# A four-layer convolution net on one core: the first image's reduce product, the bias tables and the loads at the first layer's two ends rearranged

## The chip, the cores and the metric

The kernel runs on one core of one Trainium2 chip. The metric is device time in microseconds of one execution. The engines are PE (matrix products, with PEld for its weight loads), DVE (vector), ACT (scalar), POOL (GpSimd) and SP (which here only issues DMAs). ACT and POOL issue DMAs too.

## The reference

The input is 4 images of 256 channels and 56 x 56 positions, float32. Four layers follow, each of the form x + layer(groupnorm(x)) with groups of 8 channels:

```
# layer 0 (involution): every position makes its own 7x7 kernel for each of 16 channel groups
h    = einsum('bchw,oc->bohw', xn, reduce_w) + reduce_b      # 256 -> 64 channels
kern = einsum('bchw,oc->bohw', h, span_w) + span_b           # 64 -> 49*16
out  = (kern * patches7x7(xn)).sum(axis=taps)                # 16 channels share a kernel

# layer 1: conv3x3, batch norm, relu, conv3x3, batch norm, + xn, relu
# layer 2: involution as in layer 0, with batch norm and relu after the reduce and after the sum
# layer 3: x * sigmoid(W @ first element) + x * spatial factor (both from FFTs' real parts)
```

## The kernel before

**Stages.** `involution_layer(0, ...)` does layer 0, `conv_layer` layer 1, and `involution_layer(2, ...)` layers 2 and 3. Between stages the images lie in DRAM (`stage`). Channels lie on the 128 partitions, so an image is two channel blocks `cb` of 128 x 3136 numbers, each in one of three rotating blocks of the tile named `xs` (`new_block`, L101). `new_h` (L104) gives the tile `hp`, which holds the 64 reduced channels twice, on partitions 0 to 63 and 64 to 127.

**Layer 0's units.** A unit is (image b, channel block cb), so there are eight, in order. Each has a tap phase and an output phase.

- The tap phase (`tap_matrices`, L460) runs 32 steps. A step has 6 matmuls on PE (L471) out of `z_sb` (the span weights spread over a window) and `hp`, then one eviction into `kt` that adds the bias table `zb_sb`: on DVE (L489, one instruction) or in every fourth step on ACT (L482, six instructions). `hooks` hold work to be emitted after a given step.
- The output phase (`apply`, L501) runs seven columns of 8 positions. A column has 56 matmuls (L513), evictions on ACT (L526) and DVE (L533), and an addition on POOL (L538). After each column `next_windows` (L371) transposes the strip for the third column ahead on PE (L381), ACT copies it to `xw` (L382), and three DMAs on SP and one on POOL shift it (L388, L390). `next_strip` (L345) makes the normalized strip on POOL (L364). `column_sums` (L925) takes statistics on DVE. `early` and `late` hold work placed before and after a column.

**Before the first unit.** SP loads the two blocks of image 0 in parts (`load_block`, L236). DVE takes statistics of seven chunks of each block (`sums`, L328-333). `norm_steps` (L190-213) turns them into a scale and a shift: an aggregate on DVE, two one-column matmuls with `gavg_sb` (L197, L208), small DVE steps, and `rsqrt_eps` (L137), which uses DVE and POOL. `bottleneck(0)` (L395) scales the reduce weights to `redn` (L404), makes the bias `hb` (L411-420), and multiplies (L433): for each chunk of 9 rows a half-wide matmul, two chunks side by side on the two halves, accumulated over the two channel blocks. ACT evicts a bank into one half of `hp` (L450), and DVE copies it to the other half (L441). `make_tables` (L277) loads the span and bias weights, spreads them with DVE copies (L300, L308), and makes `zb_sb` with 24 matmuls (L315) and one copy (L322). `batch_norms` (L159) folds the batch norm parameters with small DVE operations and powers on POOL.

Layer 2's tables are made in unit (0,0): `make_tables(..., nc.sync)` runs at hooks 3, 14 and 21, and `save` at 22 writes both to DRAM (L824, L825). Image 1's first block is loaded at hook 23.

**From layer 0 to layer 1.** After column 0 of the last unit `begin_conv` (L985) loads on SP the rows of image 0 for the first convolution chunk (`load_rows`, L976) and both blocks of the raw weights of the first convolution (L991). When the unit ends, the norm of its block is computed. `conv_layer` then zeroes the edges of `ph1` and `ph2` on POOL (L1079-1086), issues on ACT the loads of weight positions 0 and 5 (`row_weights`, L1046-1047), combines the raw weights on DVE (L1058-1065), normalizes the rows into four phases (`phases`, L1114, channel block 0 on ACT and 1 on DVE), transforms them on DVE (`transform`, L1136), and starts `conv1` (L1254).

**What sets the order.** The start is ordered by the framework's scheduler, which places an instruction by its dependencies and priority. From `since = mark()` on, `in_order(since)` binds each engine to the order of emission: the hooks and the lists decide. Each engine's queue is strictly in that order.

Of the kernel before, what the change touches and what calls it, by code (L numbers as in the profile page):

```python
# [16 lines left out]
P = 128  # L17
# [54 lines left out]
def net_kernel(  # L72
# [68 lines left out]
    def bn_fold(name, par, gamma, beta, mean, var, n):  # L141

        s = const.tile([P, n], F32, name=f"{name}_s")
        t = const.tile([P, n], F32, name=f"{name}_t")
        rsqrt_eps(s, par(var), BN_EPS)
        nc.vector.tensor_mul(s, s, par(gamma))
        nc.vector.tensor_mul(t, par(mean), s)
        nc.vector.tensor_sub(t, par(beta), t)
        return s, t

# [8 lines left out]
    def batch_norms():  # L159

        par_of = {}
# [8 lines left out]
        s1, t1 = bn_fold("bn1", by_channel, L1_G1, L1_B1, L1_M1, L1_V1, NB)  # L170
        s2, t2 = bn_fold("bn2", by_channel, L1_G2, L1_B2, L1_M2, L1_V2, NB)
        s4, t4 = bn_fold("bn4", by_channel, L2_G, L2_B, L2_M, L2_V, NB)
        s3, t3 = bn_fold("bn3", by_row, L2_G1, L2_B1, L2_M1, L2_V1, 1)

        s4_of = {}
        for n in (2, 4):
            s4_of[n] = const.tile([P, n, NB], F32, name=f"s4_{n}")
            for i in range(n):
                nc.vector.tensor_scalar_mul(s4_of[n][:, i, :], s4, par_of[n][:, i : i + 1])
        bn.update(par=par_of, s1=s1, t1=t1, s2=s2, t2=t2, s3=s3, t3=t3, s4=s4_of, t4=t4)  # L180
# [49 lines left out]


# [4 lines left out]
    def load_block(dst, block, parts=1):  # L236
        n = NCHUNK // parts
        for j in range(0, NCHUNK, n):
            at = slice(j * CR * W, min(j + n, NCHUNK) * CR * W)
            nc.sync.dma_start(dst[:, at], block[:, at])  # L240

    def involution_layer(layer, xin, xout, red, span, sb, xs_of, ahead=None, pending=None):

        with ExitStack() as es:
# [12 lines left out]
            def warm(n):  # L257

                ps = one_bank()
                for _ in range(n):  # L260
                    nc.tensor.matmul(ps[:, :P], ident_sb, ident_sb, start=True, stop=True)

            def load(b, cb, parts=1):
                xs_of[b, cb] = new_block()
                load_block(xs_of[b, cb], xin[b][cb], parts)

            for cb in range(NB):
                if (0, cb) not in xs_of:
                    load(0, cb, 3)

            red_sb = wpool.tile([P, NB, 2, R], F32, name="red_sb")
            for i in range(2):
                nc.scalar.dma_start(red_sb[:, :, i], red.rearrange("(cb p) r -> p cb r", p=P))
# [1288 lines left out]
```

## Time and profile before

| | |
|---|---|
| median of 3 runs | 1864.59 us (1862.81 to 1867.78) |
| profiled execution | 1861.41 us |
| its span in the trace | 1859.5 us, 55572 instructions |
| busy in the span | PE 1705.2 us (92%), DVE 1430.2 (77%), ACT 751.4 (40%), POOL 432.0 (23%) |
| moved by DMA | 215.67 MB, mean 116 GB/s |
| mean granted PE clock | 0.967 |

Layer 0 runs from the start to about 530 us; layer 1 follows, then layers 2 and 3. The page cuts the span into 40 slices of 46.5 us. In its rows a digit is the busy share in tenths, and PEclk is the clock granted to PE in tenths of full speed. In a timeline a line has start, duration, engine, source line, operation, output and input, how many instructions are merged (x), and in brackets the idle time of that engine before it and what ended it. A float32 matmul shows as two records.

### The profile page before, as it was taken

What the parts mean: (1) busy time and instruction counts of PE and PEld (TensorE: products, weight loads), DVE (VectorE), ACT (ScalarE), POOL (GpSimd) and SP (SyncE); (2) the same over time, 40 slices, a digit from 0 to 9 for tenths busy, and PEclk for the clock granted to TensorE, in tenths of its full rate; (3) what the DMA queues carried; (4) which work ended last, traced back from release to release, by engine and by line L of the source; (5) the groups of instructions that cost most, each with busy time, mean ns of one, the idle gap of its engine ahead of it and who ended that gap; (6) DMA issues with size and microseconds to landing.
All of it is one profiled execution on the core that took longest, in us unless ns stands there. A gap on an engine that the chain in (4) does not pass through costs nothing.

```text
span 1859.5 us, 55572 instructions
## 1 busy us (share of the span) xinstructions
PE 1705.2 (92%) x24028; PEld 1501.5 (81%) x24028; DVE 1430.2 (77%) x2824; ACT 751.4 (40%) x1662; POOL 432.0 (23%) x615
## 2 busy tenths in 40 slices
PE   5999999999859999999999999997989899898886
PEld 3888888888748988898899889985877887877874
DVE  5687778776668988998889888874777778778764
ACT  2445445454413222231232312113656556565543
POOL 2323433244210000000000000000000663672683
PEclk9999999999969999999999999998999999999985
DMA  3445544453543111120121111132433765763652
GB/s 100 150 147 178 154 121 138 156 154 106 159 129 101 41 62 61 61 68 25 61 71 58 51 48 33 54 122 63 154 129 127 207 209 174 201 213 118 196 164 75
DMA packets 65504, 215.67 MB, mean 116 GB/s; under 512 B 13487, under 2 KB 20444, under 8 KB 61420
## 3 DMA queue, kind: packets, MB, share of 16 engines
q1 hardware_dynamic: 44364, 141.60, 24.6%
q0 software_dynamic: 14848, 65.85, 10.9%
q10 hardware_dynamic: 6048, 4.68, 0.8%
q8 instruction: 189, 3.10, 0.7%
q14 instruction: 55, 0.45, 0.1%
HBM read 76.23 MB, written 49.15 MB: 67 GB/s over the span
## 4 chain that ended last, share of the span: by engine, by line
PE 67%; DVE 20%; DMA 4%; issue 3%; POOL 3%; ACT 2%; SPq 0%; DVEq 0%; POOLq 0%; ACTq 0%
PE mm L1336 20%; PE ps L513 15%; DVE kt L489 11%; PE mm L1254 10%; PE ps L471 8%; PE mm L1225 6%; PE ps L381 4%; DMA xw<-xw 2%; PE ps L433 2%; DVE un L533 2%; ACT hp L452 1%; DMA gx<-x 1%; PE ps L783 1%; DVE st L925 1%; DMA xs<-in_x_dram 1%
## 5 line engine op out<-in xcount | busy, mean ns | idle before, releaser
L513 PE MATMUL ps<-kt,xw 126*32 126x48 f32 (+1 forms) x12544 | 385.2, 236 | 57.0 <-DMA xw<-xw 19.2
L513 PEld LDWEIGHTS ps<-kt,xw 126*32 126x32 f32 (+1 forms) x12544 | 345.9, 122 | 102.6 <-issue 47.8
L471 PE MATMUL ps<-hp,z_sb 64*126 64x133 f32 x6144 | 387.2, 281 | 15.6 <-DVE kt L489 5.3
L471 PEld LDWEIGHTS ps<-hp,z_sb 64*126 64x126 f32 x6144 | 369.1, 188 | 30.4 <-DVE kt L489 6.6
L489 DVE TENSOR_TENSOR kt<-ps,zb_sb 126x798 f32<-126x798 f32 x384 | 357.8, 978 | 42.9 <-PE ps L471 42.4
L1336 PE MATMUL mm<-v,u_sb 128*128 128x280 f32 (+1 forms) x1728 | 383.2, 383 | 3.3 <-DVE v L1161 3.3
L1336 PEld LDWEIGHTS mm<-v,u_sb 128*128 128x128 f32 x1728 | 326.2, 189 | 57.4 <-DVE v L1161 3.6
L482 ACT ACTIVATE kt<-ps,zb_sb 126x133 f32<-126x133 f32 x768 | 224.0, 441 | 173.8 <-PE ps L471 173.8
L1254 PE MATMUL mm<-v,u_sb 128*128 128x252 f32 (+1 forms) x936 | 211.9, 387 | 12.6 <-DVE v L1145 12.6
L1254 PEld LDWEIGHTS mm<-v,u_sb 128*128 128x128 f32 x936 | 177.7, 191 | 43.1 <-issue 12.6
L533 DVE SCALAR_TENSOR_TENSOR un<-ps,par_sb,un 128x240 f32<-128x240 f32 x224 | 98.2, 456 | 101.9 <-ACT un L526 97.8
L533 DVE SCALAR_TENSOR_TENSOR un<-ps,s,un 128x240 f32<-128x240 f32 x224 | 102.4, 457 | 91.0 <-ACT un L528 86.7
L1373 POOL DMA_DIRECT2D x<-xs x24 | 13.1, 546 | 683.9 <-DVE xs L1372 538.6
L1321 ACT ACTIVATE res<-xs,shift,norm_sb 128x1120 f32<-128x1120 f32 (+1 forms) x24 | 30.2, 1259 | 234.8 <-DVE xs L1372 107.3
L538 POOL TENSOR_TENSOR xs<-un,xs 128x240 f32<-128x240 f32 x112 | 72.3, 665 | 223.0 <-DVE un L533 223.0
L382 ACT COPY xw<-ps 126x896 f32<-126x896 f32 x112 | 101.6, 907 | 50.1 <-PE ps L381 43.3
L381 PE MATMUL ps<-ident_sb,strip_sb 128*126 128x128 f32 x784 | 112.3, 284 | 1.4 <-DVE kt L489 0.8
L526 ACT ACTIVATE un<-ps,par_sb 128x240 f32<-128x240 f32 x112 | 50.1, 448 | 137.5 <-PE ps L513 134.9
L528 ACT ACTIVATE un<-ps,bn_t,s 128x240 f32<-128x240 f32 x112 | 60.1, 538 | 100.8 <-PE ps L513 94.6
L139 POOL TENSOR_TENSOR norm_sb<-norm_sb,mhalf 128x1 f32<-128x1 f32 x32 | 19.2, 602 | 351.0 <-DVE norm_sb L138 350.9
L1225 PE MATMUL mm<-xs,u_sb 128*128 128x126 f32 (+1 forms) x792 | 98.3, 277 | 1.3 <-DVE xs L1188 1.0
L1225 PEld LDWEIGHTS mm<-xs,u_sb 128*128 128x128 f32 x792 | 94.3, 191 | 2.7 <-issue 1.4
(224 smaller groups left out, 1962.3 us busy)
## 6 DMA issues: line engine op xcount, KB each, us to landing
xw<-xw SPq DMA_DIRECT2D x168, 252.0 KB
xw<-xw SPq DMA_DIRECT2D x224, 126.0 KB
xw<-xw POOLq DMA_DIRECT2D x56, 252.0 KB, 4.5
xs<-x SPq DMA_DIRECT2D x24, 560.0 KB
x<-xs POOLq DMA_DIRECT2D x8, 1568.0 KB, 8.1
xs<-x SPq DMA_DIRECT2D x8, 1568.0 KB
xs<-in_x_dram SPq DMA_DIRECT2D x6, 1568.0 KB
x<-xs SPq DMA_DIRECT2D x6, 1568.0 KB
```

The source lines that it names most:

```text
L381: nc.tensor.transpose(ps[:Q, k * P : (k + 1) * P], flat[:, k * Q : (k + 1) * Q], ident_sb)
L382: nc.scalar.copy(xw[:, :NSB, :], ps[:Q, : NSB * P].rearrange("q (n c) -> q n c", n=NSB))
L471: nc.tensor.matmul(ps[:Q, i, k * NT : (k + 1) * NT], z_sb[i * R : (i + 1) * R, cb * GB // 2 + gp, z0 : z0 + Q], hp[i * R : (i + 1) * R, py ...
L482: nc.scalar.activation(kt[:, g0 + i, pb, :, k], ps[:Q, i, k * NT : (k + 1) * NT], AF.Identity, bias=zb_sb[:, cb * GB + g0 + i, p0 + k : p0 ...
L489: nc.vector.tensor_tensor(kt[:, g0 : g0 + 2, pb], ps[:Q, :, : PB * NT].rearrange("q i (k t) -> q i t k", k=PB), zb_sb[:, cb * GB + g0 : cb ...
L513: nc.tensor.matmul(v[m * j : m * j + m, i, :, k * TP : (k + 1) * TP], xw[:, window(ty), m * j : m * j + m], kt[:, ng * j : ng * j + ng, :, ...
L528: nc.scalar.activation(part, o[0], AF.Identity, bias=bn["t4"][:, cb : cb + 1], scale=bn["s4"][ng][:, 0, cb : cb + 1])
L533: nc.vector.scalar_tensor_tensor(part, o[e], s, part, ALU.mult, ALU.add)
L538: nc.gpsimd.tensor_tensor(dst, u, dst, ALU.add)
L1225: nc.tensor.matmul(ps[:, co * m : (co + 1) * m], u[ci][:, co * P : (co + 1) * P], v2[:, e, : n // 2, ci * WT : (ci + 1) * WT], start=(ci = ...
L1254: nc.tensor.matmul(ps, u1_sb[:, ci, dy, k, co * P : (co + 1) * P], v[:, k, dy * NB + ci : (dy + n - 1) * NB + ci + 1 : NB, :], start=(j == 0),
L1336: nc.tensor.matmul(ps, u2_sb[:, ci, dy, k, co * P : (co + 1) * P], v[:, k, dy * NB + ci : (dy + n - 1) * NB + ci + 1 : NB, :], start=(j == 0),
```

## The change

- **Start.** A new generator, `begin`, runs in place of the two norms, `bottleneck(0)` and `make_tables`, now in a fixed order. The first tables come from POOL's DMA queue, with ACT making the copies and the 24 bias matmuls first on PE. Four and eight warm-up matmuls stand between the norm's matmuls. The 64-channel product is made 128 wide, by channel block: all seven chunks of block 0 into seven banks, then block 1 into the same banks. ACT evicts both halves at once, and no copies to the other half follow. The load of the image is in parts of 2, 2, 2 and 1 chunks for both blocks. The reduce weights are loaded on POOL's queue.
- **Parameters.** `batch_norms` is a generator. Two of its steps run in the start, and the rest at hooks 1, 2, 4, 6 and 7 of unit (0,0).
- **Layer 2's tables.** The span table is loaded at hook 16 of unit (3,0) and made by POOL, three copies after each of its columns 0 to 5. The bias table's matmuls run between the layers (`window_biases` in `conv_layer`).
- **Loads.** Image 1's first block is loaded at hook 16. The rows and the raw weights of channel block 1 are loaded on SP at hook 16 of unit (3,1), those of block 0 in three parts on ACT after its columns 0, 1 and 2. The loads of weight positions 0 and 5 move from ACT to SP.
- **Border.** The last block's norm moves into the first convolution stages (`slow`). All eight phases of the first chunk are made on ACT.

```diff
+    def bias_table(bias, sb, load, copy):
+        bias_g, bias_f = bias[:G, : KK * KK], bias[:G, KK * KK : KK * KK + ZN]
+        load(bias_g, sb.rearrange("(g i) k -> g i k", i=GC)[:, 0, :])
+        nc.gpsimd.memset(bias_f, 0.0)
+        yield
+        copy(field(bias_f), bias_g.rearrange("p (y x) -> p y x", y=KK))
+        yield
+
+    def window_biases(zb_sb, bias, ps):
+        bias_f = bias[:G, KK * KK : KK * KK + ZN]
+        for p in range(TP):
+            z0 = ZF - p // TX * QX - p % TX
+            nc.tensor.matmul(
+                ps[:Q, p * G : (p + 1) * G], bias_f[:, z0 : z0 + Q], ident_sb[:G, :G], start=True, stop=True
+            )
+        nc.scalar.copy(
+            zb_sb.rearrange("q g p -> q p g"), ps[:Q, : TP * G].rearrange("q (p g) -> q p g", g=G)
+        )
...
+            def begin():
+                steps = lambda g, n: [next(g) for _ in range(n)]
+                scratch = new_block()
+                n = NB * KK * KK * GB
+                biases = bias_table(scratch[:, n:], sb, nc.gpsimd.dma_start, nc.scalar.copy)
+                tables = span_table(z_sb, span, scratch, nc.gpsimd.dma_start, nc.scalar.copy)
+                next(biases)
+                next(tables)
+                load_red()
...
+                next(biases)
+                run(tables)
+                window_biases(zb_sb, scratch[:, n:], one_bank())
+                folds = batch_norms()
...
+                steps(sums0, NCHUNK)
+                norm = norm_of(0, 0, 0, sums_of[0, 0])
+                steps(norm, 2)
+                warm(4, ident_sb)
+                steps(norm, 2)
+                warm(8, ident_sb)
+                steps(norm, 1)
+                steps(sums1, 2)
+                steps(norm, 1)
+                nc.vector.tensor_scalar_mul(redn[:, 0], red_sb[:, 0], rstd[:, 0:1])
+                steps(sums1, 2)
+                next(folds)
+                steps(sums1, NCHUNK - 4)
+                pairs = [two_banks() for _ in range(4)]
+                bank = pairs[3][:, 1, :]
+                norm = norm_steps(sums_of[0, 1], lambda: bank, 0, 0, 1)
...
+                for j in range(4):
+                    products(j, 0)
+                steps(norm, 2)
+                next(folds)
+                products(4, 0)
+                steps(norm, 2)
+                next(folds)
+                products(5, 0)
+                products(6, 0)
+                steps(norm, 2)
...
+                for j in range(NH):
+                    products(j, 1)
+                for j in range(NH):
...
+                    for py in range(min(rows, TY)):
+                        dst = hp[:, py, :, a0 : a0 + n, :]
+                        nc.scalar.activation(dst, s[:, py, :, :n, :], AF.Identity, bias=hb)
+                return folds
...
+                place(hooks0, begin(), (1, 2, 4, 6, 7))
...
+                if last_image and cb == 0:
+                    g2 = tables2()
+                    place(hooks, g2, (16,))
+                elif last_image:
+                    place(hooks, g2, (1,))
+                    hooks.setdefault(16, []).append(ahead[0])
...
+                if last_image and cb == 0:
+                    for tx in range(6):
+                        late[tx] += [step(g2)] * 3
+                elif last_image:
+                    for tx in range(3):
+                        late[tx].append(ahead[1 + tx])
...
     def begin_conv():
-        room["h"] = new_h()
-        room["rows"] = new_block()
         room["v2"] = new_block()
         load_rows(0, src[1])
-        for ci, t in enumerate((room["h"], room["v2"])):
...
+        raw_weights(1, 0, 1, nc.sync)
+
+    def begin_weights(part):
+        if part == 0:
+            room["h"] = new_h()
+        raw_weights(0, part, 3, nc.scalar)
...
-                    nc.scalar.dma_start(u[:, ci, :, 0, :], w[:, :, 0, :])
-                    nc.scalar.dma_start(u[:, ci, :, 5, :], w[:, :, 2, :])
+                    nc.sync.dma_start(u[:, ci, :, 0, :], w[:, :, 0, :])
+                    nc.sync.dma_start(u[:, ci, :, 5, :], w[:, :, 2, :])
...
-            g = phases(0, nc.vector)
-            for _ in range(4):
-                next(g)
             for _ in range(NB):
                 next(weights1)
-            run(g)
+            run(phases(0))
+
+            zb2 = room["bias"][:Q, KK * KK + ZN : KK * KK + ZN + G * TP].rearrange("p (g t) -> p g t", g=G)
+            window_biases(zb2, room["bias"], one_bank())
+            nc.sync.dma_start(zb2_dram, zb2)
...
-            tail1, tail2, slow = [], [], []
+            tail1, tail2, slow = [], [], [norm_steps(st, one_bank, 1, B - 1, NB - 1)]
```

## The prediction

> **What bounds the kernel now.** I read the page's table of slices first, to find where the matrix engine is not full.
>
> ```profile
> PE   5999999999859999999999999997989899898886
> PEclk9999999999969999999999999998999999999985
> ```
>
> A slice is 46.5 us. PE is full except in slice 1 (the start), slices 11 and 12 (511 to 558 us, where layer 0 ends and the convolutions begin) and the tail. The change touches the start and that border, so I read those two stretches as timelines. Start of the kernel (start us, duration, engine, line):
>
> ```profile
> 15.86 1.68 DVE L333 BATCH_NORM_STATS2 st<-xs 128x6 f32<-128x448 f32 x3
> 17.74 0.32 DVE L194 BATCH_NORM_AGGREGATE mv<-st 128x2 f32<-128x42 f32 x1
> 22.04 0.28 DVE L404 TENSOR_SCALAR redn<-red_sb,norm_sb 128x128 f32<-128x128 f32 x1
> 23.86 6.63 PE L433 MATMUL ps<-xs,redn 128*64 128x504 f32 x26
> 26.52 6.50 ACT L450 ACTIVATE hp<-ps,hb 64x168 f32<-64x168 f32 x20 [1.03 <-PE ps L433]
> 30.42 2.81 PE L315 MATMUL ps<-ident_sb,xs 16*126 16x16 f32 x48
> 34.40 1.32 DVE L441 COPY hp<-hp 64x504 f32<-64x504 f32 x3
> 35.87 3.82 PE L471 MATMUL ps<-hp,z_sb 64*126 64x133 f32 x36 [2.63 <-DVE hp L441]
> 52.19 2.56 DVE L300 COPY xs<-xs 64x49 f32<-64x49 f32 x16
> 73.03 2.16 PE L513 MATMUL ps<-kt,xw 126*64 126x96 f32 x38 [1.06 <-DVE kt L489]
> ```
>
> The image has landed at 15.86, the second norm is folded at 22.3, and the first tap matmul runs at 35.87. Between them stand the products, 20 evictions of 0.325 us, the bias matmuls and the copies to the other half. Unit (0,0) then takes 37.2 us from its first tap to its first steady output matmul (73.03). The last unit does the same work in 25.5 us:
>
> ```profile
> 461.85 5.12 PE L471 MATMUL ps<-hp,z_sb 64*126 64x133 f32 x84
> 487.30 3.21 PE L513 MATMUL ps<-kt,xw 126*64 126x96 f32 x110 [1.05 <-DVE kt L489]
> ```
>
> Then the border, in the view of stretches (stretch, busy PE, PEld, DVE, ACT, POOL, granted clock, DMA share, GB/s) and the timeline:
>
> ```profile
> 478.00:481.00 3.00, 3.00 (x58) 3.00 (x55) 3.00 (x5) 1.75 (x6) 0.00 (x0) 1.00 0.02 5
> 505.00:508.00 3.00, 0.00 (x0) 0.00 (x0) 0.00 (x0) 0.00 (x0) 0.75 (x2) 0.77 1.01 306
> 517.00:520.00 3.00, 2.70 (x32) 2.56 (x32) 0.00 (x0) 0.00 (x0) 0.00 (x0) 0.50 0.68 179
> ```
> ```profile
> 516.18 0.59 PE L513 MATMUL ps<-kt,xw 126*64 126x96 f32 x4 [12.05 <-DMA xw<-xw]
> 534.85 1.08 ACTq L1047 DMA_DIRECT2D u_sb<-in_wc_dram  x1
> 535.98 3.36 ACT L1133 ACTIVATE ph<-xs,norm_sb 128x294 f32<-128x294 f32 x4 [7.68 <-DVE u_sb L1058]
> 540.40 2.87 DVE L1131 TENSOR_SCALAR ph<-xs,norm_sb 128x294 f32<-128x294 f32 x4
> 545.88 16.45 PE L1254 MATMUL mm<-v,u_sb 128*128 128x280 f32 x58 [12.59 <-DVE v L1145]
> ```
>
> PE stands 12.05 us for a window copy that queues behind 3.5 MB of convolution loads (two of 588 KB, two of 1152 KB, all issued from 495.2). After the last output matmul (527.7) it stands until 545.88, but for tiny norm matmuls. ACT cannot start the phases until its queue has issued four weight loads.
>
> **The change, part by part.** The sum is made against the profiled execution: 1861.41 us, of which 1859.5 are span and 1.9 lie outside. The median of the runs shown, 1864.59, is 3.2 above it. I subtract the gain from the median.
>
> *1. Time to the first tap.* First (0,0): its four parts now leave SP without the wait for gavg (4.2 us in the chain). At the 377 to 393 GB/s of 3 to 5 us, 1.6 MB land near 7.0. Seven statistics of about 0.6 us then end near 8.5 (before: 10.8). The norm chain is aggregate 0.3, matmul 0.6, four small DVE steps 0.8, matmul 0.6, and 0.2 + 0.6 + 0.2 for the root and shift: 3.3. Four warm-up matmuls stand in it. A 280-column convolution matmul takes 0.47 us at full clock (72 records, two a matmul, in 17.0 us), so 128 columns are 0.21, and 0.43 at half clock: 1.7 us against 0.8 of DVE work, so 0.9 more. Norm 0 is ready at 12.8, its weights at 13.1. Five statistics and four folds follow on DVE (3.4), so the second aggregate is near 16.9, set by DVE and not by landing, for the bytes are in by about 15 (3.86 MB at the 300 GB/s of 7 to 15 us). The products of channel block 0 lie under this: four of 0.85 us (504 columns; 1.7 at half clock) stand ahead of the second norm's matmul, 16.5 to 19.9; I take 17.2. Norm 1 adds 3.1: 20.3, and the bias matmuls bring t0 to 20.7. A 128-wide product costs double the half-wide pair (0.85 against 0.42), but only block 1's seven are on the path, and they overlap the evictions. The evictions wait for a pair of banks (1.7) and run 20 x 0.325 = 6.5. First tap near 29.0. The copies L441, the L315 matmuls and the L322 copy no longer follow. Gain 6.9; I take 6.5, because the bias load is now first in PE's queue.
>
> That queue is the unknown. The 24 bias matmuls stand ahead of everything on PE and wait for a 3 KB load from POOL's queue and an ACT copy. By the nearest row (window copies on POOL, 4.5 us median to landing) it lands near 6.5, the matmuls (2.8 us) end near 9.5 and norm 0's matmul is 0.5 late. "DMA: Bandwidth & Descriptors" of the Trainium skill (Anatomy of one DMA) gives 2.0 us plus bytes over 436 GB/s: 4 us, and no delay. Under the image load, gavg took 4.2 us; if the bias needs 8 us, 4 us are lost. ACT's table load and 17 small copies (about 0.2 us each, below its 0.29 for 133 elements) end by 12, well before evictions at 22. POOL's seven DMA issues (0.55 each) and memsets (2.3) end near 8, before the first root. Range of this part: 2.5 to 8.5.
>
> *2. Unit (0,0).* Of its 37.2 us, 2.7 are three window transposes, which stay. Removed: 24 bias matmuls of layer 2 (2.8) and the DVE stall of 16 + 2 table copies and one of 1.1, which left PE idle from 52.2 to 56.3, with the half clock behind both. Left: 25.5 + 2.7 = 28.2. The folds put about 18 small DVE operations (1.9 us with a memset) in place of the 2.2 that norms and sums take in the last unit: even. The clock decides. "TensorE: Matmul & The Clock Gate" (Part 1) says that an idle window of about 3.4 us halves the clock. The trace agrees: 0.52 at 56 to 58 us after 4 us of idle. It speaks against this change: PE finishes the products at t0 + 5.3 and the taps start at t0 + 8.3, a gap of 3.0. Under 3.4 no loss; caught by it, a further 1.75 us (3.5 us at half). I take half: 29.0, a gain of 8.2 (6 to 9).
>
> *3. The transfer stall.* Rows and one weight block (2.4 MB) move to the middle of the last unit's tap phase, the other block in three 384 KB parts behind its first three columns. "Trainium Kernel Development and Optimization" (Key Constraints) says that DMAs of SP, ACT and POOL share the same 16 engines, and other queues save only issue time. By that alone, spreading over queues gains nothing: 3.5 MB at 306 GB/s are 11.6 us wherever they collide. The row says what helps is the time: DMA share is 0.02 at 478 to 481, and there SP has no window copy until 492. Issue near 474.5, after the store that frees the block (done at 472), so landed near 482.5. Three parts beside 756 KB of window copies a 4.15 us column make 275 GB/s against the 306 seen: tight, so I leave 2 us of stall. With 0.9 for the half clock behind it and 1.1 of second wait, 14 us are at stake; gain 11.5 (8 to 13.5). ACT's issues (0.6 each) fit its 2.3 us of idle a column.
>
> *4. The gap before the first convolution.* The norm chain (530.8 to 534.3) leaves POOL and DVE and returns in later steps, 0.2 to 0.6 us an operation under 23 us convolution stages. POOL's memsets then follow the store issue at 530.95. DVE starts the weights at 531.1 and ends at 536.9 (six at 0.96). ACT no longer issues loads, so its phases start near 531.1; now eight on ACT, at 0.84 each, are 6.7: 537.8. Three DVE transforms (0.8 each) let PE start at 540.3, not 545.88. Moving four phases from DVE costs nothing as weights cover 5.8 of the 6.7. Layer 2's 24 bias matmuls fall into idle PE. The copy of their result follows the phases on ACT and the row loads follow it on SP, near 539, as before (539.4). Gain 5.5 (3 to 6.5).
>
> *5. What is added elsewhere.* POOL makes 17 table copies in unit (3,0), three a column. No row shows one; its 208-element addition takes 0.63 us, its 56-element memset 0.14. I take 0.5: 1.5 a column, against the 1.23 to 1.58 us for which POOL waits on DVE each column. Cost 0 to 3; I take 1. Behind POOL there queue the window copy and the strip that PE transposes a column later.
>
> Sum: 6.5 + 8.2 + 11.5 + 5.5 - 1.0 = 30.7. Convolution and layer 2 keep their order, so nothing gives it back: 1864.6 - 30.7 = **1834 us**.
>
> **The rivals.** *The collision stays.* Weight parts and window copies still meet in the last columns, or the store is late; only 1 to 3 of part 3 arrive: 1844. For it: 275 against 306 GB/s. Against it: most bytes land in an empty stretch. *The start gives nothing back.* Bias load late, cold clock through block 0's products and the first taps: parts 1 and 2 give 6 instead of 14.7: 1843. For it: everything on PE is queued behind one POOL load. *POOL becomes the bound, and the kernel slower.* In unit (3,0) a strided 64x49 copy costs far more than its row suggests. The 17 copies have about 8 us of slack; beyond it each us is PE's. From 2.3 us a copy (39 - 8 = 31) the change loses; at 2.6 us, 1869. Its dearest layer 0 row, the strip, takes 1.0 for 784 elements, so this is unlikely. *It doesn't do what it says:* the start was hidden by something else. The chain shows no such thing; 1862.
>
> **How the numbers follow.** My forecast 0.62 (its own range 1828 to 1841), collision 0.18, start 0.14, same 0.03, slower 0.03. 0.3% (5.6 us) is about what a measurement of this kernel can tell from no change. The range 1827 to 1848 takes in the first three, with the bounds of the parts. Faster 0.94, same 0.03, slower 0.03.
>
> **What would show it.** First tap at 27.5 to 31 us and 28 to 30 us from there to the first output; no wait over 2 us on a window copy near 490 to 510; first convolution matmul about 12.5 us after the last output matmul, not 18.2. Wrong if norm 0's matmul waits on the bias matmuls, if the clock is 0.5 through the first taps, or if PE waits for strips in unit (3,0).

## The result: 1839.64 us against 1864.56, and where the 25 us lie

The changed kernel takes 1839.64 us (median of 4 runs, 1837.56 to 1840.95), the kernel before 1864.56 (4 runs, 1862.81 to 1867.78). The ratio is 0.9854, with a 95% interval of 0.9835 to 0.9874: 24.9 us faster. A second comparison, beside the last experiments, gave 1837.36 against 1865.70, ratio 0.9855 (0.9829 to 0.9880). The forecast was 1834, with a range of 1827 to 1848. So the time lies in the range and 5.6 us above the forecast, but the parts do not lie where they were forecast. The profiled execution took 1840.73 us, 1839.0 of it span.

The table of slices of the changed kernel, PE's busy share and its granted clock in tenths:

```profile
PE   7999999999889999999999999996999899998886
PEclk9999999999989999999999999998999999999995
```

Slice 1 is fuller than before (7 for 5), and the hole at slices 11 and 12 (8 and 5 before) has become 8 and 8, with the granted clock no longer down to 6. Both stretches of the change improved. The timeline of the start shows that the first one did not do so as forecast:

```profile
7.00 10.41 PE L255 MATMUL ps<-ident_sb,xs 16*126 16x16 f32 x48 [7.00 <-ACT xs L247]
9.61 0.63 DVE L349 BATCH_NORM_STATS2 st<-xs 128x6 f32<-128x448 f32 x1 [0.74 <-DMA xs<-in_x_dram]
10.27 0.34 DVE L204 BATCH_NORM_AGGREGATE mv<-st 128x2 f32<-128x42 f32 x1
17.34 0.59 PE L207 MATMUL ps<-mv,gavg_sb 128*128 128x1 f32 x2
27.05 0.28 PE L207 MATMUL ps<-mv,gavg_sb 128*128 128x1 f32 x2
31.56 5.54 PE L520 MATMUL ps<-xs,redn 128*128 128x504 f32 x14 [0.39 <-DVE hb L548]
33.55 5.76 ACT L557 ACTIVATE hp<-ps,hb 128x168 f32<-128x168 f32 x20 [15.00 <-PE ps L520]
39.26 2.32 PE L571 MATMUL ps<-hp,z_sb 64*126 64x133 f32 x36 [2.16 <-ACT hp L557]
```

The statistics of the first block are aggregated at 10.61, not near 8.8 as forecast: the last of the seven chunks was still being awaited at 9.61, and the forecast had the whole block landed near 7.0. That is 1.8 us. The larger delay follows it. PE starts norm 0's matmul (the first L207) only at 17.34; until then it works off the 24 bias matmuls at the head of its queue, which take 10.41 us. The first tap comes at 39.26, which is 3.4 us later than before (35.87), not 6.5 earlier. The loss is mostly regained in the unit itself: its first output matmul comes at 64.97, against 71.57 before.

The end of layer 0 and the first convolution, as a timeline:

```profile
478.89 3.21 PE L613 MATMUL ps<-kt,xw 126*64 126x96 f32 x110 [1.06 <-DVE kt L589]
496.77 0.41 PE L613 MATMUL ps<-kt,xw 126*64 126x96 f32 x4 [1.04 <-DMA xw<-xw]
502.21 0.41 PE L613 MATMUL ps<-kt,xw 126*64 126x96 f32 x4 [1.42 <-DMA xw<-xw]
512.53 6.63 ACT L1240 ACTIVATE ph<-xs,norm_sb 128x294 f32<-128x294 f32 x8 [1.72 <-POOL xs L638]
515.71 1.46 SPq L1157 DMA_DIRECT2D u_sb<-in_wc_dram  x1
522.07 23.21 PE L1361 MATMUL mm<-v,u_sb 128*128 128x280 f32 x90 [3.68 <-DVE v L1252]
```

The one wait of 12.05 us is gone, and several waits up to 1.4 us stand in its place. ACT starts the phases right behind the last addition, while SP issues the weight loads. The same stretch in the view of stretches (columns as in the prediction):

```profile
494.00:497.00 3.00, 1.96 (x52) 1.49 (x40) 2.28 (x5) 1.34 (x2) 1.61 (x4) 1.00 0.92 220
500.00:503.00 3.00, 1.29 (x46) 0.83 (x36) 2.25 (x5) 0.43 (x1) 1.27 (x2) 1.00 0.90 199
```

The DMA engines are full (0.90 to 0.92) while they move only about 200 to 220 GB/s, and PE idles beside them.

The gains by stage, in us, from the timelines of three profiled executions. "Changed, again" is a second profiled execution of the same code, taken with the last experiments:

| stage | before | changed | gain | changed, again | gain | forecast |
|---|---|---|---|---|---|---|
| to the first tap | 35.87 | 39.26 | -3.4 | 38.49 | -2.6 | +6.5 |
| first tap to first output matmul | 35.70 | 25.71 | +10.0 | 27.30 | +8.4 | +8.2 |
| from there to the last unit's first output matmul | 414.27 | 412.46 | +1.8 | 410.61 | +3.7 | -1.0 |
| outputs of the last unit | 41.88 | 32.82 | +9.1 | 31.93 | +9.9 | +11.5 |
| gap to the first convolution matmul | 18.16 | 11.82 | +6.3 | 11.55 | +6.6 | +5.5 |
| first convolution matmul to the end | 1313.6 | 1316.9 | -3.3 | 1310.6 | +3.0 | 0 |

Up to the first convolution matmul the gain is 23.8 and 26.0. Behind it the code does the same work in the same order, yet two executions of one kernel differ there by 6.3 us. So a single time, and even a median of four, cannot weigh an edit of 3 us. The experiments are read by their stages, and the times stand beside them.

### The profile page after: what moved, and what is told of

Same layout as the page of the kernel before. It is cut to its first block, busy times and chain, and to the rows that moved or that the text cites. A ratio compares the mean times of both kernels' runs of the same rounds, so it can differ in the third digit from the quotient of the medians.

```text
span 1839.0 us, 55620 instructions
## 1 busy us (share of the span) xinstructions
PE 1716.7 (93%) x24052; PEld 1511.4 (82%) x24052; DVE 1413.4 (77%) x2776; ACT 760.9 (41%) x1686; POOL 441.3 (24%) x639
## 4 chain that ended last, share of the span: by engine, by line
PE 65%; DVE 21%; DMA 4%; POOL 3%; issue 3%; ACT 3%; SPq 1%; DVEq 0%; POOLq 0%; ACTq 0%
PE mm L1443 18%; PE ps L613 14%; DVE kt L589 11%; PE mm L1361 10%; PE ps L571 8%; PE mm L1332 5%; PE ps L398 4%; DMA xw<-xw 3%; PE ps L450 2%; DVE un L633 2%; DVE res L1436 1%; DMA gx<-x 1%; DVE xs L1295 1%; DVE st L1034 1%; PE ps L883 1%
## 5 line engine op out<-in xcount | busy, mean ns | idle before, releaser
L613 PEld LDWEIGHTS ps<-kt,xw 126*32 126x32 f32 (+1 forms) x12544 | 342.1, 122 | 92.4 <-issue 45.9
L571 PE MATMUL ps<-hp,z_sb 64*126 64x133 f32 x6144 | 382.5, 279 | 13.8 <-DVE kt L589 4.5
L571 PEld LDWEIGHTS ps<-hp,z_sb 64*126 64x126 f32 x6144 | 364.9, 186 | 28.5 <-DVE kt L589 5.8
```

The lines of the kernel that those rows point to most:

```text
L571: nc.tensor.matmul(ps[:Q, i, k * NT : (k + 1) * NT], z_sb[i * R : (i + 1) * R, cb * GB // 2 + gp, z0 : z0 + Q], hp[i * R : (i + 1) * R, py ...
L613: nc.tensor.matmul(v[m * j : m * j + m, i, :, k * TP : (k + 1) * TP], xw[:, window(ty), m * j : m * j + m], kt[:, ng * j : ng * j + ng, :, ...
```

## The experiments

The theories: (A) the start was lost to the bias matmuls at the head of PE's queue, slow because all 24 lie on one half of the array and because PE still has half its clock; the border was won by the time at which the loads run, and by the queue that issues them. The rivals say that the start hangs on the statistics and loads (B) or on the clock alone (C), and that the border's gain has another source. What was measured, in us:

| version | first tap | last outputs | gap | first convolution | median (range) | before beside it |
|---|---|---|---|---|---|---|
| bias matmuls on two halves | 36.43 | 31.37 | 11.82 | 519.06 | 1835.03 (1831.4 to 1837.4) | 1869.48 |
| bias matmuls behind the products | 37.36 | 32.13 | 11.91 | 520.92 | 1839.35 (1837.4 to 1841.8) | 1869.48 |
| both | 32.30 | 32.77 | 11.54 | 516.31 | 1838.23 (1827.7 to 1842.7) | 1869.48 |
| both, block 0's products late | 36.04 | 32.50 | 11.78 | 519.97 | 1836.16 (1830.8 to 1842.1) | 1869.48 |
| loads as before | 39.00 | 41.00 | 11.91 | 530.42 | 1844.77 (1843.7 to 1852.1) | 1867.08 |
| parts at columns 3 to 5 | 38.88 | 33.00 | 11.43 | 521.77 | 1839.20 (1833.8 to 1839.8) | 1867.08 |
| weight loads on ACT | 39.57 | 32.27 | 15.95 | 526.25 | 1837.75 (1835.9 to 1839.6) | 1867.08 |
| both, parts at 3 to 5 | 32.31 | 32.37 | 11.60 | 515.73 | 1832.08 (1828.1 to 1836.3) | 1867.08 |
| parts at column 6 | 39.44 | 27.94 | 16.00 | 521.94 | 1837.41 (1836.4 to 1839.2) | 1865.70 |
| both, parts at column 6 | 32.27 | 28.40 | 16.47 | 516.27 | 1829.56 (1827.8 to 1835.5) | 1865.70 |
| both, no warm-up | 33.82 | 31.67 | 11.53 | 516.57 | 1841.33 (1835.4 to 1844.5) | 1865.70 |
| the changed kernel again | 38.49 | 31.93 | 11.55 | 519.88 | 1837.36 (1832.3 to 1845.4) | 1865.70 |

### The bias matmuls: on two halves, behind the products, both

The first edit loads the bias table on two partition groups, 0 to 15 and 64 to 79, and lets the matmuls take them in turn, each half with its own bank of results, as the kernel before did. The second leaves them on one half and moves them behind the evictions of the product.

```diff
-                biases = bias_table(scratch[:, n:], sb, nc.gpsimd.dma_start, nc.scalar.copy)
+                biases = bias_halves(scratch[:, n:], sb, nc.gpsimd.dma_start, nc.scalar.copy)
...
+    def window_halves(zb_sb, bias, pair):
+        for p in range(TP):
+            k, i = divmod(p, 2)
+            half = slice(i * R, i * R + G)
+            z0 = ZF - p // TX * QX - p % TX
+            nc.tensor.matmul(
+                pair[:Q, i, k * G : (k + 1) * G], bias_f[half, z0 : z0 + Q], ident_sb[half, half],
+                start=True, stop=True,
+            )
```
```diff
                 run(tables)
-                window_biases(zb_sb, scratch[:, n:], one_bank())
                 folds = batch_norms()
...
                         nc.scalar.activation(dst, s[:, py, :, :n, :], AF.Identity, bias=hb)
+                window_biases(zb_sb, bias_sb, one_bank())
                 return folds
```

> Theory A: the start came late because the 24 bias matmuls at the head of TensorE's queue took 10.41 us instead of 2.81, by a factor of two for lying on one half of the array and another of two for the clock at the kernel's start. With two halves in turn, still first in the queue, they take 5.0-6.2 us, norm 0's first matmul starts at 12-13.5 instead of 17.34 and the first tap at 34-35.5 instead of 39.26; the time falls by 4-5 us against the changed kernel (1839.6), to about 1835. Rival C (the clock alone, the halves don't matter): still 9.5-10.5 us, first tap at 39, no gain. Rival B (the start is late by the statistics and the loads): the bias matmuls get short but the first tap stays at 38-39.5.

> The bias matmuls stay on one half but stand behind the products. Theory A: norm 0's first matmul starts at 10.6-11 (the DVE aggregate ends at 10.61), the products of block 1 about 6 us earlier (25 instead of 31.56), but the 24 bias matmuls behind them take 5-7 us on one half (6.85 at the border) and end after the evictions, so that the first tap comes at 36-37: a gain of about 3 us. Rival C (halves don't matter, clock only): 2.8-3.5 us, first tap at 33-33.5, gain 6 us. Rival B: first tap at 38-39.5, no gain.

> Both edits: bias matmuls on two halves in turn and behind the products. Theory A: norm 0's first matmul at 10.6-11, bias matmuls 2.8-3.2 us, first tap at 32.5-33.5, the time 6 us under the changed kernel (about 1833.5). Rival B: first tap at 38-39.5, no gain.

The rate of the bias matmuls, in the view of stretches for their line alone (stretch, busy PE and PEld with the records in brackets, clock, DMA share, GB/s). First the changed kernel at the start, one half:

```profile
10.00:12.00 2.00, 2.00 (x11) 2.00 (x11) 1.00 1.04 370
```

On two halves, still at the start:

```profile
10.00:12.00 2.00, 2.00 (x22) 2.00 (x22) 1.00 1.04 375
```

One half, behind the products:

```profile
32.00:34.00 2.00, 2.00 (x20) 2.00 (x20) 1.00 0.04 8
```

Two halves, behind the products (the version with block 0's products late):

```profile
34.00:36.00 2.00, 2.00 (x40) 2.00 (x38) 1.00 0.04 8
```

In 2 us run 11, 22, 20 and 40 records. So there are two factors of two, and they multiply: one for the half, one for the place in time. Rival C falls, and so does the reading that either alone explains the 10.41 us. What the edit cannot tell apart is the half from the bank, as both alternate together. The second factor is the clock. In the version with one half behind the products the clock fell while the block ran, and the view of stretches goes on there with

```profile
36.00:38.00 2.00, 1.43 (x7) 1.32 (x7) 0.50 0.00 0
```

At a granted clock of 0.50 seven records take 1.43 us, near the rate of the start (4.9 records a microsecond against 5.5). At the start itself the column has 1.00, but no record stands behind that: the first clock record of the changed kernel's trace begins at 23.85 us. The durations show the half clock before it, as the same matmul L207 takes 0.59 us at 17.34 and 0.28 at 27.05. The load of the DMA engines is not the reason: from 14 to 16 us the block still runs 11 records, at a DMA share of 0.03. "TensorE: Matmul & The Clock Gate" of the Trainium skill (Part 1) gives the half clock as the default of an idle engine, which fits these durations.

The first tap followed in part. On two halves alone the block took 0.60 + 5.29 us with 1.05 of waiting for the second load between, norm 0's matmul started at 14.04 and the first tap came at 36.43, a microsecond later than theory A's window: the clock fell to 0.56 through part of block 1's products, which took 7.24 us for 5.54. Behind the products on one half, norm 0 started at 10.95, but the block (6.75 us, as the clock fell in it) then held up the tap: 37.36, a little beyond the 36 to 37 of theory A. With both, the timeline is:

```profile
10.32 0.59 PE L207 MATMUL ps<-mv,gavg_sb 128*128 128x1 f32 x2 [10.32 <-DVE mv L204]
24.09 5.54 PE L551 MATMUL ps<-xs,redn 128*128 128x504 f32 x14 [0.39 <-DVE hb L579]
29.56 2.81 PE L269 MATMUL ps<-ident_sb,xs 16*126 16x16 f32 x48
32.30 3.78 PE L603 MATMUL ps<-hp,z_sb 64*126 64x133 f32 x36
```

Norm 0's matmul waits for nothing but its aggregate, the block takes the 2.81 us of the kernel before, and the first tap is at 32.30: 7.0 us earlier than in the changed kernel. That is theory A, and B falls as the cause of these 7.0. It keeps a part of what is still missing, since 32.30 is 2.9 us later than the forecast's tap (35.87 - 6.5 = 29.4). At the first convolution matmul 5.8 us of the 7.0 are left: the first 36 tap records take 3.78 us for 2.32, at a granted clock that falls to 0.50. The median of this version (1838.23) does not show them. Its four times scatter over 15 us, and the stages behind the first convolution matmul took 1321.4 us in its profile.

### The order by channel block

```diff
-                for j in range(4):
-                    products(j, 0)
...
-                products(4, 0)
...
-                products(5, 0)
-                products(6, 0)
...
-                for j in range(NH):
-                    products(j, 1)
+                for ci in range(NB):
+                    for j in range(NH):
+                        products(j, ci)
```

> As the version with both edits, but the seven products of block 0 run behind norm 1 with those of block 1, so the product is no longer spread by channel block; evictions between the blocks are still left out. By the trace of the changed kernel: norm 1's matmul no longer waits the 2.2 us behind products, but seven more products of 0.79 us (5.5 us) follow; the first tap comes 2.5-4 us later than in the version with both edits (at 35.5-37), the time 3 us over it. If the order by block is worth nothing, it is within 1 us of it; if it is worth all of the step's 6.5 us, 5.5-6.5 us later.

The first tap came 3.7 us later than in the version with both edits (36.04 for 32.30), and the first convolution matmul 3.7 later. So making block 0's products while block 1 is still being normalized is worth 3.7 us at the first tap. This includes a stretch at half clock (0.50 from 22 to 24 us) behind PE's wait for norm 1. The two medians do not separate. The other edits of the start (the product made 128 wide without copies, the tables from POOL's queue, the new parts of the image load) were not tried one by one.

### The loads of the convolution

```diff
-                    hooks.setdefault(16, []).append(ahead[0])
...
-                    for tx in range(3):
-                        late[tx].append(ahead[1 + tx])
+                    late[0] += ahead
...
-        raw_weights(0, part, 3, nc.scalar)
+        raw_weights(0, part, 1, nc.sync)
```

> The changed kernel with the convolution's loads (rows, the two weight blocks) all started on SyncE at the first column of the last unit's outputs, as before the change; everything else stays. Theory A (the spread of the loads is what freed the last unit's outputs): TensorE waits 11-13 us for window copies there again instead of 3.2, the outputs of the last unit take 41-43 us from the first to the last output matmul instead of 32.8, and the time is 8-10 us over the changed kernel. Rival (the wait went because the unit runs earlier or because the POOL table copies changed the window copies' timing): waits of at most 4 us, 32-34 us, no loss.

The timeline of this version:

```profile
507.43 11.08 PE L613 MATMUL ps<-kt,xw 126*64 126x96 f32 x332 [11.53 <-DMA xw<-xw]
```

The stall is back in full and in one place. The outputs take 41.0 us, the first convolution matmul comes 8.35 us later than in the changed kernel, and the time is 22.3 us under the kernel before instead of 25 to 28, so the medians show less than the 8 to 10 us that were expected. The gap behind the outputs stays at 11.9. So moving the loads is worth 8.2 us in the outputs and nothing in the gap. The rival falls.

This edit moves two things at once, the time of the loads and, for block 0's weights, the queue. The view of DMA queues of the kernel before, from 503 to 508 us inside its 12.05 us of waiting, shows that the queue matters. SP's queue is q1, POOL's is q0 (packets, MB, share of 16 engines):

```profile
q1 hardware_dynamic: 142, 1.18, 78.4%
q0 software_dynamic: 75, 0.31, 20.8%
```

By the trace's packets, practically all of the 1.18 MB on SP's queue are the weights' packets of 9216 bytes. The window copies on that queue have packets of 3072 bytes, and none of them moved, although five copies had been issued between 497.9 and 502.6 us. POOL's copies moved in the meantime, over the same engines. So the copies that PE waited for stood behind the loads in SP's own queue. Loads at the old time on another queue were not run, so how the 8.2 us divide between the time and the queue stays open.

```diff
-                        late[tx].append(ahead[1 + tx])
+                        late[3 + tx].append(ahead[1 + tx])
```

> The three parts of the weight block that ACT starts at columns 0, 1 and 2 of the last unit's outputs start at columns 3, 4 and 5. Theory A (the 3.2 us left of the stall are these parts against the window copies): the waits for window copies at 496-503 fall under 1 us, the outputs of the last unit take 29-30.5 us instead of 32.8; the gap before the first convolution matmul stays at 11.5-13 us, as the parts land before the transforms need them; first convolution matmul 2-3.5 us earlier. Rival (the 3.2 us are the window copies' own traffic): waits of 2.5-3.5 us at the same place. Second rival: the parts now meet the end, the transforms on DVE start late, and the gap grows by 2-6 us, more than is won.

Theory A was wrong about columns 3 to 5: the waits again sum to 3.2 us, now mostly one of 2.5 at 504.6, and the outputs take 33.0. What the DMA engines had to carry had moved, not shrunk. That left open whether the parts or the window copies alone fill them, so the parts were started behind the last window copy:

```diff
-                        late[tx].append(ahead[1 + tx])
+                        late[6].append(ahead[1 + tx])
```

> The changed kernel with all three weight parts started behind column 6 of the last unit's outputs, when every window copy has been started. The version with the parts at columns 3 to 5 still waited 3.2 us, now in one place (2.5 us at 504.6). Theory A (these parts' 1.18 MB share the DMA engines with the window copies wherever they overlap): now the waits for window copies fall under 0.8 us and the outputs of the last unit take 29.5-30.5 us instead of 32.8; the parts, started near 501-503, need 4-6 us at the 200-240 GB/s of this stage and land by 509, before the transforms on DVE begin, so the gap stays 11.5-12.5 and the first convolution matmul comes 2.3-3.3 us earlier than 522.07. Rival (the window copies alone fill the DMA engines): waits of 2-3.5 us stay. Second rival: the parts land after 510 and the gap grows by 1-4 us.

The view of waits and the timeline of this version:

```profile
DVE u_sb L1168 <- DMA hp<-in_wc_dram: 3.2, 1, 3.2
```
```profile
506.08 1.72 ACTq L1093 DMA_DIRECT2D hp<-in_wc_dram  x3
513.41 0.96 DVE L1168 TENSOR_TENSOR u_sb<-hp 128x768 f32<-128x768 f32 x1 [3.16 <-DMA hp<-in_wc_dram]
```

No matmul waits for a window copy any more, and the outputs take 27.94 us, 4.9 less than in the changed kernel. So the parts were the collision, and the 4.9 us are what it still costs the outputs. But the second rival decides the end: in ACT's queue the three issues stand among the last evictions and run from 506.08, not at 501 to 503. The parts land near 513.3, DVE waits 3.16 us for them, and the gap is 16.0. The first convolution matmul is at 521.94, as in the changed kernel (522.07). The stall was not removed but changed into another of the same length.

### The queue of the weight loads

```diff
-                    nc.sync.dma_start(u[:, ci, :, 0, :], w[:, :, 0, :])
-                    nc.sync.dma_start(u[:, ci, :, 5, :], w[:, :, 2, :])
+                    nc.scalar.dma_start(u[:, ci, :, 0, :], w[:, :, 0, :])
+                    nc.scalar.dma_start(u[:, ci, :, 5, :], w[:, :, 2, :])
```

> The loads of the weights by position go back from SyncE's to ACT's queue; everything else stays as in the changed kernel. In its trace the four issues took 0.64, 0.61, 1.78 and 1.46 us on SyncE, and ACT's eight phase copies (6.63 us) start at 512.53 right behind the last add. Theory A (the queue that issues them counts): the phase copies start 4-4.5 us later and end at the same delay behind the DVE's weight transforms (which end at 519.3), so that the gap before the first convolution matmul is 15.5-16.5 us instead of 11.8. Rival (the deferred normalization made the gap shorter, the queue is hidden): the gap stays within 1 us of 11.8.

```profile
515.74 1.43 ACTq L1157 DMA_DIRECT2D u_sb<-in_wc_dram  x1
517.21 6.52 ACT L1240 ACTIVATE ph<-xs,norm_sb 128x294 f32<-128x294 f32 x8 [6.35 <-issue]
```

This is the timeline of the version with the loads on ACT. The four issues run until 517.17 on ACT, the phases start at 517.21 instead of 512.53, and the gap is 15.95 us instead of 11.82. Theory A holds: 4.1 of the 6.3 us that the gap gave are the queue. The deferred norm and the rest of the border have at most the other 2.2. They were not tried alone.

### The warm-up matmuls

```diff
-                warm(4, ident_sb)
...
-                warm(8, ident_sb)
```

> As the version with the bias matmuls on two halves and behind the products, but without the 4 and 8 warm-up matmuls behind norm 0's two matmuls. Theory A (the warm-up matmuls buy the clock): TensorE's granted clock is at half through the products of block 0 and at least part of those of block 1, whose 14 matmuls took 5.54 us at full clock and then take 7-11 us; first tap 1.5-6 us later than 32.3. Rival (they only fill TensorE's queue: norm 0's second matmul and the first products stood right behind them without idle time): first tap 0.3-1 us earlier than 32.3.

The timeline of the version without them (both bias edits in it):

```profile
13.86 5.70 PE L549 MATMUL ps<-xs,redn 128*128 128x504 f32 x8 [1.56 <-DVE redn L536]
23.91 7.24 PE L549 MATMUL ps<-xs,redn 128*128 128x504 f32 x14 [0.39 <-DVE hb L577]
```

The eight records of block 0's products take 5.70 us; with the warm-up they took 3.55. The fourteen behind them take 7.24 instead of 5.54, at a clock of 0.50 to 0.71 from 24 to 28 us. That second loss need not come from the missing warm-up: with it, in the version on two halves alone, the same fourteen also took 7.24. The products start 2.3 us earlier (13.86 for 16.19), so the first tap is only 1.5 us later (33.82), at the lower end of what theory A allowed. At the first convolution matmul 0.3 us are left, and the medians do not tell the two versions apart. The warm-up is worth at most 1.5 us at the first tap in this pair of executions.

### Putting it together

The bias edits, first with the parts at columns 3 to 5, then with the parts at column 6:

> Bias matmuls on two halves and behind the products, and the weight parts at columns 3 to 5 together. If the parts add up: first tap at 32.3, outputs of the last unit 29-30.5 us, first convolution matmul at 513-514.5 against 522.07 in the changed kernel and 516.3 with the bias matmuls alone; the time 7.5-9 us under the changed kernel if the convolution layers keep it. Rival (the convolution layers scatter by more than this): the same milestones, but medians that lie within 4 us of the changed kernel's.

> The same with the bias matmuls on two halves and behind the products. If the two add up: first tap at 32.3, first convolution matmul at 513.5-514.5 (516.3 with the bias matmuls alone), 7.5-8.5 us under the changed kernel run beside it. If the convolution layers scatter more than the start gives, the medians differ by 3-8 us.

> The changed kernel itself, beside the others on the same chip, to compare them with: first tap 39.3, outputs of the last unit 32.8 us, gap 11.8, 1839-1842 us; the difference to the kernel before 24 to 28 us.

Neither met its milestone at the border (515.73 for 513 to 514.5, and 516.27 for 513.5 to 514.5). They add what the bias edits give (6 us) and nothing of the parts', for the reason shown above. Their medians, 1832.08 and 1829.56, are the lowest of all versions. The second ran beside the changed kernel on the same chip: means 1830.8 and 1838.5 of five runs each, a difference of 7.6 with a 95% interval of about 1.4 to 13.8 from the scatter of the ten times. So it is faster than both kernels; by how much is uncertain. Its first convolution matmul comes 3.6 us earlier than the changed kernel's in that comparison (519.88 - 516.27). The rest is within what the stages behind it scatter.

## Why the prediction was right, step by step

**The total.** Forecast 30.7 us, measured 24.9 and 28.3. At the first convolution matmul, where the scatter of what follows is left out, 23.8 and 26.0. The start missed by 9.9 us and the outputs by 2.4. Unit (0,0), the units behind it and the gap gave 1.8, 2.8 and 0.8 more than forecast and paid back 5.4. So the number came out right partly by luck: the 2.8 are in a stretch that nothing here explains, and the range of 21 us was wide enough to hold two of the rivals.

**The signs.** One sign of being wrong came true outright: norm 0's matmul waited on the bias matmuls. A second, half the clock through the first taps, came true in one of the two executions; PE waited for no strip in unit (3,0). Of the good signs, the first tap missed its 27.5 to 31, PE's longest wait on a window copy was 1.4 us (2.0 in the second execution), and the gap came as stated.

**Step 1, time to the first tap: wrong.** Forecast +6.5, measured -3.4. The term that failed is the one called the unknown: "it lands near 6.5, the matmuls (2.8 us) end near 9.5 and norm 0's matmul is 0.5 late". The load of the bias table was sized right, as ACT's copy of it ran from 6.71 to 6.94: near the 6.5 of the nearest row, not at the other estimate of 4. The matmuls were not: 10.41 us for 2.8. The row L315 has the same shapes and the same count, and was taken as the nearest. But it ran on alternating halves with a warm clock; the code of the change shows one half (`bias_f[:G]`), and the head of the queue means a cold engine. The range of this step (2.5 to 8.5) held a late load but not slow matmuls. They made norm 0's matmul 6.7 us late (17.34 for 10.61), and taking them away gave 7.0 of the 9.9 us back. The other 2.9 are two more terms. The image landed later than forecast, as shown above (1.8 us at the first aggregate, 1.5 in the version with both edits). And norm 1's matmul stood 2.2 us behind products (from 24.86 to 27.05; 1.7 with both edits), a wait that the forecast had put at 0.3.

**Step 2, unit (0,0): gain right, its reading of the clock wrong.** Forecast 8.2 with half of a clock loss of 1.75 us. The gap before the taps was 2.16 and 2.15 us in the two profiled executions of the changed kernel. In one the clock stayed at 1.00 (gain 10.0). In the other it fell, in the view of stretches:

```profile
39.00:41.00 2.00, 2.00 (x24) 2.00 (x23) 1.27 (x5) 0.00 (x0) 0.00 (x0) 0.54 0.00 0
41.00:43.00 2.00, 2.00 (x18) 1.76 (x16) 0.71 (x1) 1.75 (x6) 0.00 (x0) 0.61 0.03 8
```

There the gain was 8.4. So the loss is real and is not decided by the length of the gap alone. The prediction said that the trace agreed with a limit of 3.4 us, as the clock fell after 4 us of idle (52.2 to 56.3). The timeline of PE in the kernel before says otherwise:

```profile
49.60 4.44 PE L471 MATMUL ps<-hp,z_sb 64*126 64x133 f32 x72
56.27 3.86 PE L471 MATMUL ps<-hp,z_sb 64*126 64x133 f32 x36 [2.24 <-DVE kt L489]
```

PE worked until 54.04; 52.2 is where DVE turned to the table copies. The idle time was 2.24 us, and the clock fell all the same. So "under 3.4 no loss" had no support in the trace, and taking half of the loss, a fair guess, was right by luck. The page that the prediction weighed here says in the same part that the window runs freely and doesn't start with the kernel. That may be why equal gaps end differently, but no row shows the window itself, and a gap shorter than the page's window was enough here.

**Step 3, the transfer stall: the move helped as forecast, size off, one reason wrong.** Of 14 us at stake (41.88 - 27.94 = 13.9 by the version without collision) the change gave 9.1, not 11.5. The mis-sized term is the 2 us of stall left, in truth 4.9. It came from "275 GB/s against the 306 seen". Where weight parts and window copies meet (494 to 497 us), the DMA engines are 0.92 full at 220 GB/s, and where the delayed window copies run alone (500 to 503, the parts being in) 0.90 full at 199. So 306 was not to be had. One of the prediction's own lines pointed there: 179 GB/s at a share of 0.68 come to 263 at a full share. The rival of the collision was partly true. The wrong reason is that spreading over queues gains nothing because the engines are shared: by the view of queues above, sharing the engines slowed POOL's copies (8.9 us to landing, 4.5 as a rule) but did not stop them, and sharing a queue stopped SP's.

**Step 4, the gap: right.** Forecast 12.6 us, measured 11.8 and 11.55. The share of the queue that issues the weight loads is shown (4.1 us); the rest of the gain was not taken apart.

**Step 5, POOL's table copies: cost nothing.** Forecast 1.0. In the timeline of POOL in unit (3,0):

```profile
429.67 1.00 POOL L381 TENSOR_SCALAR strip_sb<-xs,norm_sb 128x784 f32<-128x784 f32 x1
430.62 0.69 POOL L338 COPY xs<-xs 64x49 f32<-64x49 f32 x3
431.94 1.29 POOL L638 TENSOR_TENSOR xs<-un,xs 128x240 f32<-128x240 f32 x2 [0.63 <-DVE un L633]
```

Three copies take 0.69 us, 0.23 each for the 0.5 taken, and POOL still waits 0.63 us for DVE behind them. PE waits for no strip in this unit. What the stretch gained instead (1.8 and 3.7 us) is not explained; no experiment went after it. Part of it can be scatter: over all versions with the change the stretch took 410.4 to 413.9 us, and the kernel before has one trace (414.27).

**The rivals.** "The start gives nothing back" gave parts 1 and 2 together 6; they gave 6.6 and 5.8. Its outcome for these parts came true and its first mechanism did not: the load of the bias table was on time. Its sentence "everything on PE is queued behind one POOL load" names the right place. The slower case (from 2.3 us a copy) was far off.

## What to carry to other kernels

A row of a profile prices an instruction only in its state: before using it for a moved or rewritten instruction, compare the partitions and banks it touches (the row's shape doesn't tell) and whether the engine is warm there. What stands at the head of an engine's queue is paid by everything behind it, so work whose result is needed last belongs behind the chain that leads to the first result. Before a stall is counted as won, ask when the moved transfer must have landed: loads that collide with one reader and are late for the next only swap one wait for another. Ask too what stands in the same queue ahead of the transfer that is waited for.

## What the hardware showed that was not expected

- Float32 matmuls of 16 rows by 126 columns on one half and into one bank ran at half the rate of the same matmuls in turn on two halves and two banks: 11 against 22 records in 2 us at the kernel's start, 20 against 40 at full clock.
- The clock column had 1.00 throughout the start, while the same matmul took 0.59 us there and 0.28 ten microseconds later. Before the first clock record (23.85 us in the changed kernel) the column measures nothing.
- The 24 small matmuls did not bring up the clock, though they filled PE from 7.00 to 17.41: the first record of full clock came at 23.85, 6.1 us after the first warm-up matmul. Behind the products on one half, the clock fell to 0.65 and 0.50 (34 to 38 us) while they filled PE.
- Two executions of the same code, with gaps of 2.16 and 2.15 us on PE, differed in whether about 3.5 us at half clock followed. In the version with both bias edits no gap stood between the products and the taps, only the 24 small matmuls, and the clock fell to 0.50 all the same.
- DMA engines at a share of 0.90 moved 199 GB/s with a backlog of copies within SBUF alone, at 0.92 220 GB/s where these mixed with weight loads, and 370 GB/s at the start of the kernel at a share of 1.04.
- For 5 us a queue with 3.5 MB of loads ahead moved none of the copies behind them, while a copy on another queue went through the same engines.
